# One attention step in eight multiplied in float32 on half-width column tiles

## The chip, the core and the metric

The kernel runs on one core of a Trainium2 chip. The core has five engines that run side by side: PE (TensorE, matrix products into PSUM), DVE (VectorE), ACT (ScalarE), POOL (GpSimd) and SP (SyncE, which here only issues DMAs). Data moves between memory and the core's SBUF by 16 DMA engines. Products land in PSUM, which has eight banks of 512 float32 columns by 128 partitions. The metric is the device time of one execution in microseconds; the profiled execution also gives a span, from its first to its last instruction.

## What is computed

A transformer layer and then a graph attention layer, for 2 sequences of 2048 rows of 512 features, all in float32. The change lies in the first layer's attention (16 heads of 32 features):

```python
q = heads(x @ Wq + bq)
k = heads(x @ Wk + bk)
v = heads(x @ Wv + bv)
scores = jnp.einsum('bhqd,bhkd->bhqk', q, k) / np.sqrt(HD)
attn = jax.nn.softmax(scores, axis=-1)
out = jnp.einsum('bhqk,bhkd->bhqd', attn, v)
...
x = x + out.reshape(B, L, D) @ Wo + bo
mlp = gelu(ada_ln(x, cond, Wln2, bln2) @ W1 + b1) @ W2 + b2
x = x + mlp
```

Each of the 32 (sequence, head) pairs needs 2048 x 2048 scores, their exponentials, and the product of these with the values. The MLP and the graph attention follow.

## The kernel before

**Stages.** A first stage makes the layer norm, the queries, keys and values of the first sequence. Then comes the attention of all 32 pairs, with other work (projections of later heads, the second sequence's norm, the output product of the first sequence) threaded in as a "background" that advances a set number of steps per unit (`PACES`). Then the MLP, and then the graph attention.

**A unit.** A pair has four query blocks of 512, and a query block has eight steps, each with two key tiles of 128. One step is a unit, `u`; there are 32 x 32 = 1024 of them. In unit `u`, `attend` records:

- two score products of 512 columns (`scores`, tile `st`), each into one of three banks, and two exponentials on ACT (`exponents`, tile `e`), which leave float32 exponentials in SBUF;
- two products for the bounds of a later pair's scores (`pair_scores`, tile `mx`), one activation on ACT (`magnitude`, tile `ab`) and one reduction on DVE (`largest`, tile `sums`);
- every fourth unit, one DMA issued by POOL that reads four units of float32 exponentials and writes them back as float16 (`high_parts`, `eh`);
- nine units later, the rest `el = e - eh` in float16, cut along its columns: one part on DVE, the other on POOL (`low_parts`; `SHARES` sets the cut);
- eleven units later, the product with the values (`weigh`): for each of the two key tiles and four groups of 128 queries, `eh` as weights against 65 columns (a column of ones, the high half of the values, their low half) and `el` against 33 (ones and the high half). These 16 matmuls add up in one bank, `av`, over the eight steps. After the eighth, DVE sums the halves, divides by the column of sums and SP stores the result.

**What sets the order.** Every engine call is recorded in the class `Order`, which knows what each reads and writes. `flush` then lays the calls out by a list schedule: a cost for each call (`cost`), a latency from engine to engine, and earlier recorded calls first among those that are ready. Each engine runs its own list in that order, on whose emission nearly all instructions have one line, L269; groups are therefore told apart by their tiles. Calls inside `order.together` stay next to each other; others may be parted. Where a POOL call with two SBUF operands follows a DVE call of that sort, `flush` makes POOL wait for it, so that the two halves of `el` take turns.

**Memory.** `places` gives each tile name a ring of slots in SBUF, and `bank` does so for PSUM. The exponentials `e` have three slots of four units each. All eight PSUM banks are given away: `s0`, `s1`, `s2` to the scores, `x0`, `x1`, `x2` to the bounds, `av` and `misc`.

Of the kernel before, what the change touches and what calls it, by code (L numbers as in the profile page):

```python
# [11 lines left out]
F32 = mybir.dt.float32  # L12
# [10 lines left out]
P = 128  # L23
B, S, D = 2, 2048, 512
KC = D // P
# [9 lines left out]
M = 20  # L35
# [12 lines left out]

EQ = 4

PACES = {0: 0.9, 1: 1.25, 2: 1.25, 17: 0.8, 18: 0.42, 28: 0.55}
# [261 lines left out]
def cost(engine, name, out, ins, kw):  # L313

    n = math.prod(c for _, c in out.ap[1:])
    if name == "dma_start":
        sizes = [mybir.dt.size(a.dtype) for a in (out, ins[0])]
        total = math.prod(c for _, c in out.ap) * max(sizes)
        row = min(a.ap[-1][1] * z if a.ap[-1][0] == 1 else z for a, z in zip((out, ins[0]), sizes))
        row = min(row, 16384)  # L320
        after = total / row * (9 + row / 24.5) / 16
        return (470.0, DONE + after) if engine == "SP" else (1040.0, DONE + 690.0 + after)
    pointers = sum(math.prod(c for _, c in a.ap[1:]) == 1 for a in ins) if n > 1 else 0
    n_in = max([n] + [math.prod(c for _, c in a.ap[1:]) for a in ins])
    psum = any(getattr(a.tensor, "space", None) == PSUM for a in ins)
    if engine == "PE":
        wide = ins[0].dtype == F32
        passes = 1 if not wide else 2 if name == "transpose" else 4
        return max(25.0, n * 0.4167 * passes + 2.7), 0.0
    if engine == "ACT":  # L330
        return (52 if psum else 93) + 0.8325 * n + 93 * min(pointers, 1), 0.0
    if engine == "POOL":
        return (36 + 0.83 * n, 0.0) if not ins else (161 + 0.833 * n, 0.0) \
            if name == "tensor_scalar" else (146 + (1.89 if out.dtype != F32R else 2.1) * n, 0.0)
    fast = name in ("tensor_copy", "tensor_scalar", "memset") and not psum
    return 66 + (0.525 if fast else 1.05) * n_in + 60 * min(pointers, 2), 0.0
# [28 lines left out]
def places():  # L365
# [8 lines left out]
        "wg_b": ["w1"], "x_a": w((7, 9), (2, 4)), "vs_a": ["w4", "eh2", "w0"],  # L374
        "hf_a": ["el0", "el1"], "kf_a": ["h8", "el3"], "hh0": h((0, 4)), "hl0": h((4, 8)),
        "hh1": ["eh0"], "hl1": ["eh1"], "ones": ["el2"],
# [5 lines left out]
        "vs": w((4, 5)), "bv": ["vf1"], "bo": w((6, 7)), "qk2": w((15, 17)), "u2": ["h9"],  # L382
        "wg": w((5, 7)), "x": w((7, 9)), "kf": ["h8"], "uf": ["l1"], "vf": ["vf0"], "qf": ["vf0"],
        "hf": ["vf0"],
        "m2": ["m2_0", "m2_1"], "m1": ["m1_0", "m1_1"], "tr": ["tr_0", "tr_1"],
# [3 lines left out]
        "wo": [f"v{i}" for i in range(4)], "xr": ["vf0", "vf1"], "ob": ["h8", "h9"],  # L389
        "oo2": w((15, 17)), "x1_a": w((7, 9)), "ob_b": ["l9"], "oo2_b": ["v2"],  # L390

        "w": w((4, 6), (7, 9), (2, 4), (14, 15), (11, 13), (9, 10), (15, 17), (10, 11), (13, 14),
               (0, 2)),
        "w8": ["eh0", "eh1"], "w16": q, "gh": h((0, 4), (8, 9)), "gl": h((4, 8), (9, 10)),
        "x1": ["v0", "v1"], "hf_m": ["v3"], "wr": ["ab0", "ab1"] + el[2:4], "gf": el[0:2],
        "g2": ["eh2"], "b2": w((6, 7)), "res": el[2:4] + ["ab0", "ab1"],

        "wbl": ["l0"], "ai": ["l1", "vf0", "vf1"], "af": ["l2"], "cv": ["l3"], "lab1": ["l4", "l5", "l6", "l7"],
        "cvt": ["l8"], "oo": ["l9"],
        "fw": ["vf0", "vf1"], "fv": ["ab0", "ab1"], "fs": ["v2"], "fq": ["l0", "l1", "l2", "l3"],  # L400
        "ws": ["ab0", "ab1"] + el[2:4], "ft": ["v2"],
        "kbd": ["l4", "l5", "l6", "l7"], "gc": ["l4", "l5", "l6", "l7"], "kv": ["l8"], "kh": ["m1_0", "m1_1"],

# [7 lines left out]
def transformer_then_graph_attention(  # L411
# [20 lines left out]
    bank = Slots(order, ps_pool, {  # L432
        "up": ["s0", "s1", "s2", "av", "misc"], "late": ["av", "misc"], "st": ["s0", "s1", "s2"], "mx0": ["x0", "x1"],
        "mx1": ["x2"], "ph": ["x1", "x2", "av"], "gs": ["misc", "s0", "s1"], "gp": ["s2", "x0"],
# [22 lines left out]
    def mm3(acc, lh, ll, rh, rl, start, stop):  # L457
# [14 lines left out]
    gsum = fixed([P, B * NT], "gsum")  # L472
    x40 = fixed([P, KC, B, M], "x40")

# [5 lines left out]
    h_dram = [[dram.tile([2, KC, P, TB], F32, name=f"h_{b}_{tb}", tag=f"h_{b}_{tb}")  # L480
               for tb in range(NTB)] for b in range(1)]
    v_dram = [dram.tile([S, H * VC], F16, name=f"v_{b}", tag=f"v_{b}") for b in range(B)]
    o_dram = [[dram.tile([S, P], F32, name=f"o_{b}_{g}", tag=f"o_{b}_{g}")
# [198 lines left out]

    def norm_block(ps, xt, ln, b, name, hi, lo, tag, stats=None, lows=(V, G)):

# [29 lines left out]
    def first_norm(b, tb, ps, xt, fast, to, stats=None):  # L714
        to[b, tb] = features(b, tb, tb % 2 if fast else 0, "")
        hi, lo = to[b, tb]
        yield from norm_block(ps, xt, 0, b, f"a{b}_{tb}", lambda c: hi[c], lambda c: lo[c],
                              "hf_a" if fast else "hf", stats)
        for v in range(2 if b == 0 else 0):
            if fast and tb % 2:  # L720
                Q.dma_start(out=h_dram[b][tb][v].rearrange("c p t -> p c t"), in_=whole[v].bitcast(F32))
            else:
                for c in range(KC):
                    Q.dma_start(out=h_dram[b][tb][v, c], in_=to[b, tb][v][c].bitcast(F32))
# [8 lines left out]
    def project(b, tb, ps, hi, lo, fast, groups=range(NG), values=True):  # L733
# [72 lines left out]
        def finish_v(t, pp):  # L806
            vs = sb("vs_a" if fast else "vs", [P, H, VC], F16, f"vs_{b}_{tb}_{t}")
            v3 = pp.rearrange("p (h d) -> p h d", d=HD)

            def high():  # L810
                copy(A, vs[:, :, 1:1 + HD], v3)
                G.memset(vs[:, :, 0:1], 1.0)
# [42 lines left out]
    for i in range(2):  # L855
        G.memset(hl_p[i], 0.0)

    heads = [(b, h) for b in range(B) for h in range(H)]
    N = len(heads) * NU
    gates = {}  # L860
    pe = {}
    va, m2s, sts, avs, mxs = {}, {}, {}, {}, {}
    es, ehs, els = [], [], {}

# [20 lines left out]
    def load_values(b, g):  # L885
        va[b, g] = [sb("va" if i < 2 else "va_rest", [P, min(VT, NT - VT * i), 4 * VC], F16,
                       f"va_{b}_{g}_{i}") for i in range(-(-NT // VT))]
        for i, t in enumerate(va[b, g]):
            r = slice(VT * i * P, min(VT * i + VT, NT) * P)
            Q.dma_start(out=t, in_=v_dram[b][r, g * 4 * VC:(g + 1) * 4 * VC]  # L890
                        .rearrange("(t p) c -> p t c", p=P))


# [63 lines left out]
    def high_parts(i):  # L957

        G.dma_start(out=ehs[i % 3], in_=es[i % 3])

    def low_parts(u):
# [3 lines left out]
        G.tensor_tensor(el[:, cd:], e[:, cd:], eh[:, cd:], ALU.subtract)  # L965
        V.tensor_tensor(el[:, 0:cd], e[:, 0:cd], eh[:, 0:cd], ALU.subtract)

    def weigh(u):
# [4 lines left out]
        if kp == 0:  # L973
            avs[0] = bank("av", [P, 4, VC + 1], F32, f"av_{n}_{qb}")
        av = avs[0]
        with order.together("PE"):
            for a in range(2):
                kt = 2 * kp + a
                v = va[b, g][kt // VT][:, kt % VT, hh * VC:(hh + 1) * VC]
                for q in range(4):  # L980
# [4 lines left out]
                    T.matmul(av[:, q, 0:1 + HD], lhsT=el[:, qs], rhs=v[:, 0:1 + HD],  # L985
                             start=False, stop=(kp == 7 and a == 1 and q == 3),
                             skip_group_check=True)
        if kp < 7:
            return
# [37 lines left out]
    def attend(n, work=None):  # L1027

        for u in range(n * NU, (n + 1) * NU):
            i, m = u % NU, u + NU  # L1030
            for a in range(2):
                exponents(2 * u + a)
                if 2 * u + a + 3 < 2 * N:
                    scores(2 * u + a + 3)
            if m < N:
# [5 lines left out]
            if u % EQ == 0 and u:  # L1041
                high_parts(u // EQ - 1)
            if u >= LOW:
                low_parts(u - LOW)
            if u >= WEIGH:
                weigh(u - WEIGH)
# [89 lines left out]

    def second_norm(ps, i, xtag, tag):
        xt = [load(sb(xtag, [P, 2, D], F32, f"x1_{i}_{j}"),
# [5 lines left out]
        def new(to, name):  # L1144
# [3 lines left out]
        yield from norm_block(ps, xt, 1, i // NTB, f"m{i}", lambda c: new(hi, "gh"),  # L1148
                              lambda c: new(lo, "gl"), tag, lows=(V, V))

# [57 lines left out]
    for i in range(3):  # L1208
        es.append(sb(f"q{i}", [P, EQ, 2 * TB], F32, f"e_{i}"))
    for i in range(3):  # L1210
        scores(i)
    beside(some(2, (), True, late), (), 1)
    beside(some(3, (), True, late), (), 1)
    load_values(0, 0)
    for i in range(3):
        ehs.append(sb(f"eh{i}", [P, EQ, 2 * TB], F16, f"eh_{i}"))
# [43 lines left out]
    def from_half():  # L1260
# [3 lines left out]
        yield from output(misc, 0, range(NG), bo_b)  # L1264
        yield from second_norm(misc, 0, "x1_a", "hf")

    works = {0: to_half, 17: from_half, 28: lambda: output(misc, 1, range(NG - 1), from_half.bo_b)}
    for n in range(len(heads)):
# [5 lines left out]
        attend(n, work)  # L1274
    high_parts(N // EQ - 1)
    for u in range(N - WEIGH, N):
        if u + WEIGH - LOW < N:
            low_parts(u + WEIGH - LOW)
        weigh(u)
    work.rest()  # L1280
# [97 lines left out]
    def folded():  # L1378
# [27 lines left out]
        for d in range(2):  # L1406
            for c in range(KC):
# [11 lines left out]
                for fc in range(KC):  # L1419
# [4 lines left out]
                                ALU.add)  # L1424

        g40 = fixed([2, B, M], "g40")
        G.memset(g40, 1.0)
# [15 lines left out]
        for b in range(B):  # L1443
            Q.dma_start(out=rows[b][0:1], in_=cond_dram[b:b + 1])
            Q.dma_start(out=rows[b][1:2], in_=brows[0:1])
        kv = sb("kv", [P, KC, B, M], F32, "kv")
        for fc in range(KC):
# [120 lines left out]
    for i in range(B * NTB):  # L1568
        hi, lo = h2.pop(i)
        nxt = second_norm(misc, i + 1, "x1", "hf_m") if i + 1 < B * NTB else None  # L1570
        held = None
# [216 lines left out]
```

## Time and profile before

| | us |
|---|---|
| median of three runs | 3416.27 (3414.47 to 3421.3) |
| the profiled execution | 3414.05 |
| its span | 3412.0 |
| PE busy in the span | 3183.1 (93%) |
| DVE busy | 2353.7 (69%) |
| ACT busy | 2058.3 (60%) |
| POOL busy | 1536.9 (45%) |

The costliest groups of the attention stage. Each line of the page names the engine, the operation, the tile written and the tiles read, their shape and count, then the busy time and the mean of one in ns, then how long the engine had been idle just before them and what ended most of that.

```profile
L269 POOL TENSOR_TENSOR el<-e,eh 128x496 f16<-128x496 f32 (+2 forms) x1024 | 1153.3, 1146 | 518.7 <-DVE el L269 378.9
L269 ACT ACTIVATE e<-st 128x512 f32<-128x512 f32 x2048 | 1153.6, 618 | 156.5 <-PE st L269 66.0
L269 DVE TENSOR_TENSOR el<-e,eh 128x528 f16<-128x528 f32 (+2 forms) x1024 | 784.5, 810 | 9.3 <-PE av L269 8.9
L269 PE MATMUL av<-va,eh 128*128 128x65 f16 x8192 | 622.9, 193 | 5.4 <-DVE os L269 4.8
L269 PE MATMUL av<-va,el 128*128 128x33 f16 x8192 | 599.6, 181 | 25.1 <-POOL el L269 12.4
```

A matmul's mean is its latency, not the time until the next can start: matmuls overlap, so 8192 of 193 ns have only 622.9 us of busy time between them. The page's DMA part gives the cast `eh<-e` 256 issues of 1024 KB, 8.3 us each from issue to landing, and its queue 40.9% of the time of the 16 DMA engines over the span.

### The profile page before, as it was taken

Reading aid. Unit: us, or ns where it says so; the run is one execution under the profiler, and the core shown is the slowest. Engines: PE = TensorE matmul, PEld = TensorE weight load, DVE = VectorE, ACT = ScalarE, POOL = GpSimd, SP = SyncE. Lnnn points to the kernel's source line nnn. Section 1 sums busy time; section 2 is a strip of 40 time slices with the busy share of each in tenths; the row PEclk is TensorE's granted clock in tenths of the full one; section 3 lists DMA queues with packets and bytes.
Section 4 is the critical chain, followed back from the end, with each engine's and each line's share of the span. In section 5 each row is a group of like instructions: output and inputs, shape, how many; then the busy total and the mean of one; then the engine's idle time right before and its main releaser. Section 6 shows DMA issues by size and latency. Waiting matters only on the chain. (4 is left out here: it accounts for less than half of the span.)

```text
span 3412.0 us, 75509 instructions
## 1 busy us (share of the span) xinstructions
PE 3183.1 (93%) x28042; PEld 2114.2 (62%) x28042; DVE 2353.7 (69%) x5372; ACT 2058.3 (60%) x3984; POOL 1536.9 (45%) x1568
## 2 busy tenths in 40 slices
PE   7988889999999999899998999879999999999999
PEld 5555545555555445455554455558888878788887
DVE  6777667888888887788888887764676324235554
ACT  5777778888888888788888887632221212112111
POOL 2254556666666776676776676641000000003222
PEclk9998999999999999899999999889999999999999
DMA  8998999898989889899998899872222164231111
GB/s 288 266 240 224 233 230 221 188 228 186 219 196 201 173 182 187 176 203 205 190 201 162 162 194 195 189 215 91 63 67 62 33 213 145 64 101 53 56 55 45
DMA packets 358238, 563.35 MB, mean 165 GB/s; under 512 B 127983, under 2 KB 234007, under 8 KB 325102
## 3 DMA queue, kind: packets, MB, share of 16 engines
q0 software_dynamic: 36864, 268.45, 40.9%
q1 hardware_dynamic: 321006, 290.08, 27.7%
q8 instruction: 220, 3.60, 0.4%
q14 instruction: 148, 1.21, 0.1%
HBM read 198.45 MB, written 91.45 MB: 85 GB/s over the span
## 5 line engine op out<-in xcount | busy, mean ns | idle before, releaser
L269 POOL TENSOR_TENSOR el<-e,eh 128x496 f16<-128x496 f32 (+2 forms) x1024 | 1153.3, 1146 | 518.7 <-DVE el L269 378.9
L269 ACT ACTIVATE e<-st 128x512 f32<-128x512 f32 x2048 | 1153.6, 618 | 156.5 <-PE st L269 66.0
L269 DVE CUSTOM_DVE_ANT_0 sums<-mx,ab 128x512 bf16<-128x512 f32 x1024 | 703.4, 687 | 264.6 <-ACT ab L269 203.0
L269 PE MATMUL st<-qst,kst 98*128 98x512 f16 x2048 | 737.4, 389 | 79.1 <-ACT e L269 44.4
L269 DVE TENSOR_TENSOR el<-e,eh 128x528 f16<-128x528 f32 (+2 forms) x1024 | 784.5, 810 | 9.3 <-PE av L269 8.9
L269 ACT ACTIVATE ab<-mx 128x512 f32<-128x512 f32 x1024 | 631.7, 617 | 152.4 <-PE mx L269 131.1
L269 PEld LDWEIGHTS <-eh 128*128 128x128 f16 x8192 | 548.7, 99 | 200.0 <-issue 149.8
L269 PE MATMUL av<-va,eh 128*128 128x65 f16 x8192 | 622.9, 193 | 5.4 <-DVE os L269 4.8
L269 PE MATMUL av<-va,el 128*128 128x33 f16 x8192 | 599.6, 181 | 25.1 <-POOL el L269 12.4
L269 PEld LDWEIGHTS <-el 128*128 128x128 f16 x8192 | 514.9, 97 | 143.8 <-DVE el L269 30.4
L269 PE MATMUL mx<-ust,qst 96*128 96x512 f16 x1024 | 396.0, 387 | 36.9 <-ACT ab L269 23.2
L269 PE MATMUL mx<-kst,qst 96*128 96x512 f16 x1024 | 389.0, 388 | 43.5 <-DVE m L269 41.9
L269 PEld LDWEIGHTS <-qst 96*128 96x128 f16 x2048 | 193.0, 98 | 346.5 <-issue 258.9
L269 ACT ACTIVATE gf<-ph,b_c 128x512 f32<-128x512 f32 x128 | 88.1, 689 | 467.1 <-PE ph L269 406.5
L269 PE MATMUL ph<-gh,w 128*128 128x512 f32 x1024 | 346.5, 400 | 3.1 <-ACT w L269 1.4
L269 PEld LDWEIGHTS <-kst 98*128 98x128 f16 x2048 | 171.4, 98 | 221.6 <-issue 176.9
L269 POOL TENSOR_TENSOR res<-res,b_b 128x512 f32<-128x512 f32 x32 | 42.7, 1348 | 570.2 <-DVE g L269 269.4
L269 PE MATMUL po_s<-w,g 128*128 128x512 f32 x1152 | 297.4, 398 | 0.0
L269 PEld LDWEIGHTS po_s<-w,g 128*128 128x128 f32 x1152 | 214.1, 188 | 49.5 <-issue 2.7
L269 POOL DMA_DIRECT2D eh<-e x256 | 146.2, 571 | 218.2 <-ACT e L269 80.0
L269 DVE CAST g<-gf 128x512 fp32r<-128x512 f32 x128 | 56.4, 441 | 254.5 <-PE po_x L269 243.5
L269 PEld LDWEIGHTS ph<-gh,w 128*128 128x128 f32 x1024 | 192.2, 189 | 51.2 <-issue 3.2
(257 smaller groups left out, 4039.2 us busy)
## 6 DMA issues: line engine op xcount, KB each, us to landing
eh<-e POOLq DMA_DIRECT2D x256, 1024.0 KB, 8.3
wg<-w SPq DMA_DIRECT2D x56, 512.0 KB
x<-in_x SPq DMA_DIRECT2D x24, 512.0 KB
qst<-qk SPq DMA_DIRECT2D x192, 64.0 KB
kst<-qk SPq DMA_DIRECT2D x192, 64.0 KB
x<-xr SPq DMA_DIRECT2D x48, 256.0 KB
v<-vs SPq DMA_DIRECT2D x32, 260.0 KB
qk<-q SPq DMA_DIRECT2D x32, 256.0 KB
```

Of the source, the lines that this page charges most:

```text
L269: ins = call(*args, **kw)
```

## The change

The last of the eight steps of each query block (`KX = 7`) leaves the scheme of high and low parts:

- its exponentials stay float32; the cast of every second group of four units takes three units instead of four, and the step has no `low_parts` and no `weigh`;
- three units after the step, `weigh_whole` multiplies in float32 the other way round: the values (33 columns: ones and 32 features) are the weights, 256 queries stream. The first key tile's result goes to partitions 0 to 32, the second's to 64 to 96, of one bank, `ot`, so the two use different 64-column tiles of the array. Four matmuls, not kept together, and one ACT copy of the 97 x 512 result to SBUF (`xo`, one slot);
- four float32 matmuls in the seventh step's `weigh`, kept together, take `xo` as weights and a 97 x 33 matrix `pick` (two identities, one below the other) as the moving operand. They turn the result round, add the two halves and accumulate into `av`;
- the float32 values of those two key tiles are copied and stored when they are made (`vx`), and loaded per group of four heads (`xa`);
- `ot` takes the bank `s2`, so the scores have two banks, and `scores` is recorded two ahead of the exponentials instead of three;
- the planner's cost counts a float32 matmul of 256 columns at 2.2 passes;
- to find room in SBUF, unused names are dropped from `places` and five tiles used after attention (`cvt`, `oo`, `kv` with `x40`, `ob_b`) move to slots that others also use.

```diff
+KX = 7
+XLAG = 3
...
         passes = 1 if not wide else 2 if name == "transpose" else 4
+        if wide and n == TB // 2:
+            passes = 2.2
...
-        "up": ["s0", "s1", "s2", "av", "misc"], "late": ["av", "misc"], "st": ["s0", "s1", "s2"], "mx0": ["x0", "x1"],
+        "up": ["s0", "s1", "s2", "av", "misc"], "late": ["av", "misc"], "st": ["s0", "s1"], "ot": ["s2"], "mx0": ["x0", "x1"],
...
+            if (tb * TB // P + t) // 2 == KX:
+                vx = sb("vx", [P, D], F32, f"vx_{b}_{t}")
+                A.copy(vx, pp)
+                Q.dma_start(out=vx_dram[b][t % 2 * P:(t % 2 + 1) * P], in_=vx)
...
+        for a in range(2):
+            Q.dma_start(out=xas[g % 2][:, a, :, 1:1 + HD],
+                        in_=vx_dram[b][ts(a, P), ts(g, P)].rearrange("p (h d) -> p h d", d=HD))
...
-        G.dma_start(out=ehs[i % 3], in_=es[i % 3])
+        n = EQ - (i * EQ % 8 + EQ > KX)
+        G.dma_start(out=ehs[i % 3][:, 0:n], in_=es[i % 3][:, 0:n])
...
+    def weigh_whole(u):
+
+        n, qb = u // NU, u % NU // 8
+        b, h = heads[n]
+        ot = ots[0]
+        for i in range(2):
+            for a in range(2):
+                T.matmul(ot[a * P // 2:a * P // 2 + 1 + HD, ts(i, TB // 2)],
+                         lhsT=xas[h // 4 % 2][:, a, h % 4],
+                         rhs=es[u // EQ % 3][:, u % EQ, a * TB + i * TB // 2:][:, 0:TB // 2],
+                         start=True, stop=True)
+        xo = xos[n, qb] = sb("xo", [XR, TB], F32, f"xo_{n}_{qb}")
+        A.copy(xo, ot[0:XR])
...
+        if kp == KX - 1:
+            xo = xos.pop((n, qb))
+            with order.together("PE"):
+                for q in range(4):
+                    T.matmul(av[:, q, 0:1 + HD], lhsT=xo[:, ts(q, P)], rhs=pick, start=False,
+                             stop=False, skip_group_check=True)
...
-                if 2 * u + a + 3 < 2 * N:
-                    scores(2 * u + a + 3)
+                if 2 * u + a + 2 < 2 * N:
+                    scores(2 * u + a + 2)
...
-            if u >= LOW:
+            if u >= LOW and (u - LOW) % 8 != KX:
                 low_parts(u - LOW)
-            if u >= WEIGH:
+            if u >= XLAG and (u - XLAG) % 8 == KX:
+                weigh_whole(u - XLAG)
+            if u >= WEIGH and (u - WEIGH) % 8 != KX:
                 weigh(u - WEIGH)
```

More of the change, by code (lines that the diff above doesn't have):

```diff
@@ L374, in places @@
         "wg_b": ["w1"], "x_a": w((7, 9), (2, 4)), "vs_a": ["w4", "eh2", "w0"],
-        "hf_a": ["el0", "el1"], "kf_a": ["h8", "el3"], "hh0": h((0, 4)), "hl0": h((4, 8)),
+        "hh0": h((0, 4)), "hl0": h((4, 8)),
         "hh1": ["eh0"], "hl1": ["eh1"], "ones": ["el2"],
@@ L382, in places @@
         "vs": w((4, 5)), "bv": ["vf1"], "bo": w((6, 7)), "qk2": w((15, 17)), "u2": ["h9"],
-        "wg": w((5, 7)), "x": w((7, 9)), "kf": ["h8"], "uf": ["l1"], "vf": ["vf0"], "qf": ["vf0"],
-        "hf": ["vf0"],
+        "wg": w((5, 7)), "x": w((7, 9)), "uf": ["l1"], "vx": ["h8"], "xo": ["xo"],
         "m2": ["m2_0", "m2_1"], "m1": ["m1_0", "m1_1"], "tr": ["tr_0", "tr_1"],
@@ L389, in places @@
         "wo": [f"v{i}" for i in range(4)], "xr": ["vf0", "vf1"], "ob": ["h8", "h9"],
-        "oo2": w((15, 17)), "x1_a": w((7, 9)), "ob_b": ["l9"], "oo2_b": ["v2"],
+        "oo2": w((15, 17)), "x1_a": w((7, 9)), "ob_b": ["l0"], "oo2_b": ["v2"],
         "w": w((4, 6), (7, 9), (2, 4), (14, 15), (11, 13), (9, 10), (15, 17), (10, 11), (13, 14),
@@ L394, in places @@
         "w8": ["eh0", "eh1"], "w16": q, "gh": h((0, 4), (8, 9)), "gl": h((4, 8), (9, 10)),
-        "x1": ["v0", "v1"], "hf_m": ["v3"], "wr": ["ab0", "ab1"] + el[2:4], "gf": el[0:2],
+        "x1": ["v0", "v1"], "wr": ["ab0", "ab1"] + el[2:4], "gf": el[0:2],
         "g2": ["eh2"], "b2": w((6, 7)), "res": el[2:4] + ["ab0", "ab1"],
         "wbl": ["l0"], "ai": ["l1", "vf0", "vf1"], "af": ["l2"], "cv": ["l3"], "lab1": ["l4", "l5", "l6", "l7"],
-        "cvt": ["l8"], "oo": ["l9"],
+        "cvt": ["v3"], "oo": ["v2"],
         "fw": ["vf0", "vf1"], "fv": ["ab0", "ab1"], "fs": ["v2"], "fq": ["l0", "l1", "l2", "l3"],
         "ws": ["ab0", "ab1"] + el[2:4], "ft": ["v2"],
-        "kbd": ["l4", "l5", "l6", "l7"], "gc": ["l4", "l5", "l6", "l7"], "kv": ["l8"], "kh": ["m1_0", "m1_1"],
+        "kbd": ["l4", "l5", "l6", "l7"], "gc": ["l4", "l5", "l6", "l7"], "kv": ["v3"], "kh": ["m1_0", "m1_1"],
         "x2t": ["vf0", "vf1", "ab0", "ab1"], "oos": ["l0", "l1", "l2", "l3"], "sc": ["v0", "v1", "v2"],
@@ L472, in transformer_then_graph_attention @@
     gsum = fixed([P, B * NT], "gsum")
-    x40 = fixed([P, KC, B, M], "x40")
     qk_dram = [[dram.tile([2, D, S], F16, name=f"qk_{b}_{w}", tag=f"qk_{b}_{w}")
@@ L481, in transformer_then_graph_attention @@
                for tb in range(NTB)] for b in range(1)]
+    vx_dram = [dram.tile([2 * P, D], F32, name=f"vx_{b}", tag=f"vx_{b}") for b in range(B)]
     v_dram = [dram.tile([S, H * VC], F16, name=f"v_{b}", tag=f"v_{b}") for b in range(B)]
@@ L681, in transformer_then_graph_attention, with norm_block @@
     HOLD = "hold"
-    def norm_block(ps, xt, ln, b, name, hi, lo, tag, stats=None, lows=(V, G)):
+    def norm_block(ps, xt, ln, b, name, hi, lo, stats=None):
         if stats is None:
@@ L717, in first_norm @@
         yield from norm_block(ps, xt, 0, b, f"a{b}_{tb}", lambda c: hi[c], lambda c: lo[c],
-                              "hf_a" if fast else "hf", stats)
+                              stats)
         for v in range(2 if b == 0 else 0):
@@ L856, in transformer_then_graph_attention @@
         G.memset(hl_p[i], 0.0)
+    xas = [fixed([P, 2, 4, 1 + HD], f"xa_{i}") for i in range(2)]
+    for i in range(2):
+        G.memset(xas[i], 1.0)
+    XR = P // 2 + 1 + HD
+    pick = fixed([XR, 1 + HD], "pick")
+    G.memset(pick, 0.0)
+    for r in (0, P // 2):
+        G.tensor_copy(pick[r:r + 1 + HD], ident[0:1 + HD, 0:1 + HD])
     heads = [(b, h) for b in range(B) for h in range(H)]
@@ L862, in transformer_then_graph_attention @@
     va, m2s, sts, avs, mxs = {}, {}, {}, {}, {}
-    es, ehs, els = [], [], {}
+    es, ehs, els, xos, ots = [], [], {}, {}, []
     def put(dst, src, low):
@@ L966, in low_parts @@
         V.tensor_tensor(el[:, 0:cd], e[:, 0:cd], eh[:, 0:cd], ALU.subtract)
+    def weigh_whole(u):
+        n, qb = u // NU, u % NU // 8
+        b, h = heads[n]
+        ot = ots[0]
+        for i in range(2):
+            for a in range(2):
[5 more added lines that the diff above has]
+        A.copy(xo, ot[0:XR])
     def weigh(u):
@@ L985, in weigh @@
                     T.matmul(av[:, q, 0:1 + HD], lhsT=el[:, qs], rhs=v[:, 0:1 + HD],
-                             start=False, stop=(kp == 7 and a == 1 and q == 3),
+                             start=False, stop=(kp == KX - 1 and a == 1 and q == 3),
                              skip_group_check=True)
-        if kp < 7:
+        if kp < KX - 1:
             return
@@ L1135, in transformer_then_graph_attention, with second_norm @@
     h2 = {}
-    def second_norm(ps, i, xtag, tag):
+    def second_norm(ps, i, xtag):
         xt = [load(sb(xtag, [P, 2, D], F32, f"x1_{i}_{j}"),
@@ L1148, in second_norm @@
         yield from norm_block(ps, xt, 1, i // NTB, f"m{i}", lambda c: new(hi, "gh"),
-                              lambda c: new(lo, "gl"), tag, lows=(V, V))
+                              lambda c: new(lo, "gl"))
     h1 = {}
@@ L1209, in transformer_then_graph_attention @@
         es.append(sb(f"q{i}", [P, EQ, 2 * TB], F32, f"e_{i}"))
-    for i in range(3):
+    for i in range(2):
         scores(i)
@@ L1214, in transformer_then_graph_attention @@
     load_values(0, 0)
+    ots.append(bank("ot", [P, TB], F32, "ot"))
+    V.memset(ots[0], 0.0)
     for i in range(3):
@@ L1264, in from_half @@
         yield from output(misc, 0, range(NG), bo_b)
-        yield from second_norm(misc, 0, "x1_a", "hf")
+        yield from second_norm(misc, 0, "x1_a")
     works = {0: to_half, 17: from_half, 28: lambda: output(misc, 1, range(NG - 1), from_half.bo_b)}
@@ L1275, in transformer_then_graph_attention @@
     high_parts(N // EQ - 1)
+    weigh_whole(N - 1)
     for u in range(N - WEIGH, N):
-        if u + WEIGH - LOW < N:
-            low_parts(u + WEIGH - LOW)
-        weigh(u)
+        low = u + WEIGH - LOW
+        if low < N and low % 8 != KX:
+            low_parts(low)
+        if u % 8 != KX:
+            weigh(u)
     work.rest()
@@ L1424, in folded @@
                                 ALU.add)
+        kvx = sb("kv", [P, 2, KC, B, M], F32, "kvx")
+        kv, x40 = kvx[:, 0], kvx[:, 1]
         g40 = fixed([2, B, M], "g40")
@@ L1445, in folded @@
             Q.dma_start(out=rows[b][1:2], in_=brows[0:1])
-        kv = sb("kv", [P, KC, B, M], F32, "kv")
         for fc in range(KC):
@@ L1569, in transformer_then_graph_attention @@
         hi, lo = h2.pop(i)
-        nxt = second_norm(misc, i + 1, "x1", "hf_m") if i + 1 < B * NTB else None
+        nxt = second_norm(misc, i + 1, "x1") if i + 1 < B * NTB else None
         held = None
```

## Prediction

> **What bounds the kernel now.** I read the page's slices first, then a table of stages, then single tiles in one stage, then the order of single instructions. The slices split the run in two. Up to slice 27 all five engines and the DMA engines are loaded; after it PE alone is full. The table of stages (us, then busy time and instructions of PE, weight loads, DVE, ACT, POOL, then granted clock, DMA share, GB/s) says it in numbers:
>
> ```profile
> 600.00:800.00 200.00, 188.93 (x2128) 114.00 (x2127) 164.06 (x378) 169.49 (x341) 124.88 (x133) 1.00 0.90 203
> 1200.00:1400.00 200.00, 183.49 (x2235) 103.98 (x2233) 162.83 (x385) 168.84 (x335) 134.66 (x143) 0.96 0.89 184
> 2600.00:2800.00 200.00, 200.00 (x875) 153.51 (x874) 81.09 (x238) 39.57 (x57) 10.39 (x8) 1.00 0.37 114
> ```
>
> The exponentials run from 127.1 to 2232.3 us and the last subtraction is at 2254, so attention is a stage of 2127 us for 1024 units (a unit: 512 queries against two key tiles), 2.08 us each. The change touches only this stage.
>
> PE's busy time there cannot be used as it stands: it holds the pipeline's latency. The order of instructions gives the spacing of starts, which is what a matmul really takes from PE:
>
> ```profile
> 1003.50 0.38 PE L269 MATMUL mx<-ust,qst 96*128 96x512 f16 x1
> 1003.72 0.38 PE L269 MATMUL mx<-kst,qst 96*128 96x512 f16 x1
> 1003.93 0.20 PE L269 MATMUL av<-va,eh 128*128 128x65 f16 x1
> ...
> 1004.39 0.48 PE L269 MATMUL misc<-hh,wg 128*128 128x512 f32 x1
> ```
>
> A 512-column half-precision matmul takes 0.2165 us, the 16 value matmuls of a unit 0.46 us together (1003.93 to 1004.39, 28.5 ns each), a 512-column background matmul 0.2325 us. Now the same stage, tile by tile (st: PE, ACT; mx: PE, DVE, ACT; misc: PE, loads, DVE, ACT):
>
> ```profile
> 600.00:800.00 200.00, 64.12 (x191) 110.66 (x191) 1.00 0.90 203
> 600.00:800.00 200.00, 63.16 (x193) 65.61 (x96) 60.13 (x97) 1.00 0.90 203
> 600.00:800.00 200.00, 63.81 (x208) 35.84 (x208) 22.37 (x36) 24.36 (x41) 1.00 0.90 203
> ```
>
> (191 + 193) x 0.2165 + 95.5 units x 0.456 + 208 x 0.2325 = 83 + 44 + 48 = 175 us of 200: PE streams 88% of the time where background work is heavy. From 1200 to 1400 the same sum gives 151 us, 79% at its clock of 0.96. Over the stage: 4096 score and bound matmuls 887, values 467, background and the rest about 336, together 1690 us; at the mean clock of about 0.97 that is 1742 us, 82% of 2127.
>
> Nobody else is slack. The two halves of the subtraction el = e - eh take turns on DVE and POOL: DVE's median is 0.697 us, four POOL halves in a row took 4.38 us, so 0.65 + 1.10 = 1.75 us of each 1.87 us unit between 1200 and 1400. ACT is 84 to 87% busy, DMA 89 to 95%. So the stage is balanced: PE is nearest to its end from 600 to 1000 us, the subtraction's turns from 1200 to 1400, DMA before 600 us (0.92 to 0.95).
>
> **What the change takes away**, once per query block (128 of them). Sixteen value matmuls: 128 x 0.456 = 58 us of PE. One subtraction: 128 x 1.14 us of POOL and 128 x 0.77 us of DVE, an eighth of the turns (1.75 falls to 1.53 us per unit). A quarter of every second cast: the cast's queue holds 40.9% of 3412 us for 256 issues, 5.45 us each, so 128 x 5.45 / 4 = 174 us of all 16 DMA engines, 8 points of the stage. These are real reliefs, but of resources beside PE.
>
> **What it adds to PE.** No float32 product of this shape is in the trace, but two near rows are:
>
> ```profile
> 2858.60 1.91 PE L269 MATMUL misc<-fv,kv 128*40 128x512 f32 x4
> 2860.45 0.50 PE L269 MATMUL ph<-gh,w 128*128 128x512 f32 x1
> 2814.15 0.98 PE L269 MATMUL misc<-kv,fw 128*128 128x40 f32 x8
> 2814.96 0.48 PE L269 MATMUL po_s<-w,g 128*128 128x512 f32 x1
> ```
>
> Each float32 matmul is two records. The first row: 4 records of 512 columns, started about 0.44 us apart, so a record takes two passes. With 256 columns a record is 0.2165 us and a matmul 0.433 us; four per block are 1.73 us one after another. They sit on two halves of the columns and may overlap. The Trainium skill ("TensorEngine Tiling (Array Packing)", Key Properties) says that different tiles execute in parallel, but that a change of the tiling mode drains the engine. By its first half the 512 matmuls cost 512 x 0.2165 = 111 us. Its second half speaks against this change: in the order in which the changed program is built, the four are not kept together. I count 331 separate runs of them among full-width matmuls: 222 single ones, 61 pairs, 24 triples, 24 complete fours. The two records of one matmul use the same half and cannot overlap, so I count two slots of 0.2165 for a single, three for a pair, four for a triple, five for four: 96 + 40 + 21 + 26 = 183 us. The trace has a case of the change of mode: the 40-column group is entered and left about 0.1 us late each time (2860.45 against 2858.60 + 4 x 0.4267 = 2860.31). A 36-row matmul in the last stage (3108.79) loses some 0.3 us in both together. 331 x 0.25 = 83 us. Sum 266 us; between 121 us (the changed program's own planner counts 0.237 us per matmul, and no drain) and 219 + 99 = 318 us (no overlap). I take 266, because the built order, not the ideal four, is what runs.
>
> The small products: 512 float32 matmuls, 97 rows by 128 weights, 33 columns. The second row is nearly this shape: 8 records, four matmuls, took 0.81 us to the next start, and 1.01 us by their weight loads. I take 0.9: 128 x 0.9 = 115 us (104 to 129). The planner's formula gives them 0.06 us each, so bundles of 0.9 us stand in PE's order as if they were 0.23 us, and the score matmuls behind them come late.
>
> PE in all: 266 + 115 - 58 = **+323 us**, 0.32 us per unit (167 to 389). From 600 to 800 us, 95.5 units would then need 175 + 30 = 205 us of PE in 200 us: longer even on a PE that never waits. From 1200 to 1400: 151 + 34 = 185 us, at its clock 193 of 200. So PE is the bound nearly everywhere.
>
> **What it adds to ACT.** 128 copies of 97 x 512 from PSUM, as the casts of this size, 0.60 us: 77 us, ACT's stage sum from about 1780 to 1857 us, 87%. Behind each copy stand the next exponentials; the copy waits for the last of the four matmuls, placed about four units after the block's exponentials end.
>
> **Two score banks instead of three.** A bank's round is exponential 0.60, score 0.39 and two handovers, which no row shows alone; at some 0.25 us each, an estimate from the gaps about them, 1.5 us for two exponentials, against 1.87 us per unit. Alone it fits; with a 0.9 us bundle or a drained group ahead of the score it does not, and ACT waits. Bounds: nothing, to 0.2 us per unit (205 us). I take nothing beside the PE bound, since PE is then the later of the two, and keep the rest as a rival.
>
> The rest: four value copies and their stores and 16 small loads on SP's queue (64 KB each, like the 384 query and key loads already there), a few fills before the stage; 0 to 3 us. The moved slots (labels, folded weights, last output) are used where PE is at 200.00 of 200 and the other engines below two thirds; that hides a wait there, and without cover it is a few us.
>
> **Sum.** The stage's PE work is 1690 + 323 = 2013 us, 2075 at clock 0.97. At 100% that is still under 2127, so the result hangs on how full PE can be. The fullest windows reach 88 to 89% today; with subtraction and DMA relieved I take 93%: 2231 us, +104. Profiled execution: 3414.05 (span 3412.0 and 2 around it) + 104 = 3518; the median of the three runs is 2 us above it, so **3520**. At 97% it is +12 (3428), at 89% +204 (3620): the likeliest case's own range.
>
> **Rivals.**
> (a) PE becomes the bound, as above: 3520, chance 0.60.
> (b) Relief wins: the halves overlap fully and drains hide, PE gains only 167 us, (1690 + 167) / 0.97 / 0.97 = 1974 us; then ACT decides, 1857 us at 90% = 2063, so -64: 3352. For it: the subtraction's turns (94% of a unit in the quiet windows) and DMA at 0.95 early. Against: 222 singles, and 600 to 1000 us where PE leads already. It decides only if the four matmuls cost under about 1.2 us per block with all drains. Chance 0.13.
> (c) Both sides cancel, within 7 us of 3416: 0.05.
> (d) Two banks starve ACT on top of (a): another 0.12 us per unit, +123: 3643. For it: ACT already waits 66 us for scores and 131 us for bounds. Against: ACT has 13% to spare. Chance 0.22.
> This kernel's runs lie within 0.2% (7 us) of each other, which is what counts as no change. Faster 0.13, same 0.05, slower 0.82. The range 3400 to 3660 leaves out most of (b) and the upper third of (d).
>
> **What would show it.** After: the attention stage ends near 2360 us; single 256-column records 0.21 to 0.22 us apart, pairs not doubling; groups of pick near 0.9 us; PE's idle share down, DVE and POOL lower, DMA share near 0.8; longer ACT waits for st. Wrong if the stage shortens, or if four products with their drains take under 1.2 us.

## The result and the profile after

The changed kernel takes 3429.22 us in the median of nine runs (3426.9 to 3431.23), the kernel before 3416.27 us in nine runs beside it (3408.68 to 3423.0). The ratio is 1.0039, with a 95% interval of 1.0028 to 1.005: slower by 13 us, where the prediction said 104 us and a range from 3400 to 3660.

The table of stages of the changed kernel, for the windows shown of before (us, then busy time and instructions of PE, weight loads, DVE, ACT and POOL, then clock, DMA share, GB/s):

```profile
600.00:800.00 200.00, 198.15 (x2051) 119.66 (x2050) 154.54 (x352) 170.59 (x344) 106.75 (x115) 1.00 0.82 186
1200.00:1400.00 200.00, 192.06 (x2141) 105.98 (x2142) 145.82 (x361) 169.56 (x336) 115.01 (x125) 1.00 0.79 160
```

PE is busier (198 of 200 us against 189), DVE and POOL are less busy, the DMA share fell from 0.90 to 0.82, and the granted clock, the share of full TensorE speed that the chip allowed, is higher (over the attention stage 0.981 in place of 0.959). The groups of the page say the same:

```profile
L273 ACT ACTIVATE e<-st 128x512 f32<-128x512 f32 x2048 | 1162.2, 617 | 182.9 <-PE st L273 160.5
L273 POOL TENSOR_TENSOR el<-e,eh 128x496 f16<-128x496 f32 (+2 forms) x896 | 1000.4, 1132 | 537.0 <-DVE el L273 238.3
...
L273 DVE TENSOR_TENSOR el<-e,eh 128x528 f16<-128x528 f32 (+2 forms) x896 | 701.0, 814 | 14.3 <-POOL el L273 7.1
...
L273 PE MATMUL av<-va,el 128*128 128x33 f16 x7168 | 512.2, 180 | 2.9 <-DVE el L273 1.7
...
L273 PE MATMUL ot<-e,xa 128*33 128x256 f32 x1024 | 228.7, 392 | 1.4 <-ACT e L273 1.4
```

Read the ends of the lines. PE hardly waits for el any more (2.9 us before these matmuls against 25.1). ACT now waits 160.5 us for scores, against 66.0. That alone does not make PE the late engine, since two score banks without the rest of the change already raise this wait to 134.2 us (experiment 2). The stage, from the first exponential to the end of the last value matmul, took 2148 us against 2129; what follows is the same length within 2 us.

What the new products take from PE is in the order of instructions. Each float32 matmul is two records. A single matmul (x2), a pair (x4) and a whole four (x8), in three cut-outs of the changed kernel's PE:

```profile
1079.39 0.39 PE L273 MATMUL mx<-ust,qst 96*128 96x512 f16 x1
1079.71 0.62 PE L273 MATMUL ot<-e,xa 128*33 128x256 f32 x2
1080.27 0.60 PE L273 MATMUL st<-qst,kst 98*128 98x512 f16 x2
```

```profile
1112.85 0.38 PE L273 MATMUL mx<-kst,qst 96*128 96x512 f16 x1
1113.16 0.63 PE L273 MATMUL ot<-e,xa 128*33 128x256 f32 x4
1113.72 0.39 PE L273 MATMUL mx<-ust,qst 96*128 96x512 f16 x1
```

```profile
1096.44 0.38 PE L273 MATMUL mx<-kst,qst 96*128 96x512 f16 x1
1096.75 1.06 PE L273 MATMUL ot<-e,xa 128*33 128x256 f32 x8
1097.74 0.73 PE L273 MATMUL misc<-wv,hh 128*128 128x512 f32 x2
```

The start of a group comes 0.31 us after the 512-column matmul ahead of it, where 0.215 us is usual: 0.094 us lost on entry. From there to the next start a single takes 0.56 us and a pair 0.56: the second half of the columns is free. Over all groups of the trace the medians are 0.552 us for 222 singles, 0.559 for 61 pairs, 0.984 for 24 triples and 0.991 for 24 fours. With the entry, 0.646, 0.653, 1.078 and 1.085 us; by the means, 238 us in all. So a four costs less than two singles (1.085 against 1.292 us), and the 222 single matmuls of the 512 run as if there were no second half. The small products:

```profile
1111.16 0.98 PE L273 MATMUL av<-pick,xo 97*128 97x33 f32 x8
1111.97 0.20 PE L273 MATMUL av<-va,eh 128*128 128x65 f16 x1
```

Four of them (8 records) take 0.81 us in the median, 0.84 on average, 108 us in all.

### The profile page after: what moved, and what is told of

Read it like the earlier page. It is cut to its first block, busy times and chain, and to the rows that moved or that the text cites. A ratio compares the mean times of both kernels' runs of the same rounds, so it can differ in the third digit from the quotient of the medians.

```text
span 3429.5 us, 75869 instructions
## 1 busy us (share of the span) xinstructions
PE 3327.5 (97%) x28041; PEld 2201.5 (64%) x28042; DVE 2259.7 (66%) x5245; ACT 2117.1 (62%) x4117; POOL 1384.1 (40%) x1445
## 5 line engine op out<-in xcount | busy, mean ns | idle before, releaser
L273 ACT ACTIVATE e<-st 128x512 f32<-128x512 f32 x2048 | 1162.2, 617 | 182.9 <-PE st L273 160.5
L273 POOL TENSOR_TENSOR el<-e,eh 128x496 f16<-128x496 f32 (+2 forms) x896 | 1000.4, 1132 | 537.0 <-DVE el L273 238.3
L273 PE MATMUL st<-qst,kst 98*128 98x512 f16 x2048 | 720.6, 385 | 38.4 <-ACT e L273 27.1
L273 DVE TENSOR_TENSOR el<-e,eh 128x528 f16<-128x528 f32 (+2 forms) x896 | 701.0, 814 | 14.3 <-POOL el L273 7.1
L273 ACT ACTIVATE ab<-mx 128x512 f32<-128x512 f32 x1024 | 637.2, 622 | 71.0 <-PE mx L273 67.2
L273 PEld LDWEIGHTS <-eh 128*128 128x128 f16 x7168 | 473.9, 98 | 131.1 <-issue 86.0
L273 PE MATMUL av<-va,eh 128*128 128x65 f16 x7168 | 528.8, 192 | 0.5 <-DVE os L273 0.5
L273 PE MATMUL av<-va,el 128*128 128x33 f16 x7168 | 512.2, 180 | 2.9 <-DVE el L273 1.7
L273 PEld LDWEIGHTS <-el 128*128 128x128 f16 x7168 | 443.0, 96 | 96.3 <-DVE el L273 9.0
L273 PE MATMUL ot<-e,xa 128*33 128x256 f32 x1024 | 228.7, 392 | 1.4 <-ACT e L273 1.4
```

The source lines that it names most:

```text
L273: ins = call(*args, **kw)
```

## The experiments

In each, the kernel before ran on the same chip; its medians there were 3415 to 3419 us, and "less" and "more" are against these. The diffs are cut (`...`), some lines to the part that differs.

**1. The four products together.**

```diff
+        with order.together("PE"):
             for i in range(2):
                 for a in range(2):
                     T.matmul(ot[...
```

> The changed kernel with its four float32 matmuls of a block kept together, nothing else. Measured in the changed kernel's trace (start of the group to start of the next matmul, plus 0.094 us lost on entry): a single costs 0.646 us, a pair 0.653, a triple 1.078, a four 1.085. All fours would cost 128 x 1.085 = 139 us of PE against 238 now, 99 us less. Theory P (PE is the bound of the changed kernel, 92% full): the time falls by 50 to 100 us, to 3330 to 3380. Rival B (the two score banks hold ACT back, PE is only busy beside it): no change or a loss, 3420 to 3450, since a group of 1.1 us now stands ahead of a score. Rival R (the other engines are just as tight, so PE time is not worth its own length): a gain of under 30 us, 3400 to 3425.

3370.08 us (ratio to before 0.9863, 0.9841 to 0.9884): 59 us under the changed kernel for 99 us less of PE. So PE time counts in the changed kernel, at about 60% of its length, and the version is faster than both kernels (45 us under the one before). All 128 groups of eight records take 0.991 us in the median.

**2. Two score banks alone**, on the kernel before.

```diff
-"st": ["s0", "s1", "s2"]
+"st": ["s0", "s1"]
...
-                    scores(2 * u + a + 3)
+                    scores(2 * u + a + 2)
```

> The kernel before with two score banks instead of three and scores recorded two ahead, nothing else of the change. Theory P: the lookahead costs little, 0 to 20 us, 3416 to 3436. Rival B: it costs 40 us or more, 3456 and up, and then the change without it would have been faster than before.

3445.1 us (1.0085, 1.0061 to 1.0109), 30 us more, between the two expectations. The table of waits (who waited for whom: us in total, times, longest) shows the way it takes:

```profile
ACT e L269 <- PE st L269: 134.2, 228, 4.2
```

In the kernel before this wait was 66.0 us in 92 waits.

**3 and 4. The relief without the price, and the price without the relief.** The third run takes `weigh_whole` and the small products out of the changed kernel; the fourth puts the old treatment of the eighth step back beside the new.

```diff
 # 3
-            if u >= XLAG and (u - XLAG) % 8 == KX:
-                weigh_whole(u - XLAG)
...
-        V.reciprocal(rec, av[:, :, 0])
+        V.tensor_scalar(rec, av[:, :, 0], 0.0, 1.0, ALU.mult, ALU.add)
 # 4
-        n = EQ - (i * EQ % 8 + EQ > KX)
+        n = EQ
...
-            if u >= LOW and (u - LOW) % 8 != KX:
+            if u >= LOW:
```

> The changed kernel without the float32 products: no four matmuls, no copy of their result, no small products; the last step's share is left out of the sums, and the division by them with it (a copy of the same size stands there). What is left is the relief alone, with two banks: PE 1690 - 58 = 1630 us, ACT 1780, an eighth less of subtraction and casts. Theory P: the relief is worth something of its own, 3250 to 3330 (the stage falls by 90 to 170 us), and the products then cost 100 to 180 us. Rival R: the relief is worth nearly nothing since ACT and the score loop hold the stage, 3370 to 3416, and the products cost only 15 to 60 us.

> The changed kernel with the old treatment of the last step put back beside the new one, so that this step is counted twice in the sums: the price without the relief. PE 1690 + 346 = 2036 us. If the relief of the subtraction and the casts is what let PE fill (theory P as the prediction had it, with 88 to 90% as the fullest), 3560 to 3640. If PE can fill to 92% without any relief (its waits were slack all along), 2036 / 0.92 = 2213 us of stage, 3500 at most; under 3470 if it fills to 95%.

The relief alone: 3282.55 us (0.9614, 0.9585 to 0.9643), 133 us less. The price alone: 3602.74 us (1.0542, 1.0514 to 1.057), 188 us more. These two large effects make up the small result: the products cost 147 us where the relief is present (3282.55 to 3429.22), and the relief is worth 174 us where the products are (3602.74 to 3429.22).

How full PE was can be compared over the stage. PE's work is estimated from the products' measured prices, 28.5 ns per value matmul and the 1690 us of the prediction for the rest. The last column divides the share by the clock that was granted over the stage.

| version | PE work, us | stage, us | share | granted clock | share of what was granted |
|---|---|---|---|---|---|
| before | 1690 | 2129 | 79% | 0.959 | 83% |
| relief alone (3) | 1632 | 2000 | 82% | 0.969 | 84% |
| price alone (4) | 2045 | 2324 | 88% | 0.976 | 90% |
| both | 1978 | 2148 | 92% | 0.981 | 94% |
| both, four together (1) | 1879 | 2086 | 90% | 0.980 | 92% |

**5 and 10. The planner's costs.** Costs as measured, with the four together (5) and without (10):

```diff
         if wide and n == TB // 2:
-            passes = 2.2
+            passes = 2.5
+        if wide and n == 1 + HD:
+            passes = 15.5
```

> The changed kernel with its four float32 matmuls together, and with the planner's costs set to what the trace shows: 2.5 passes for a 256-column float32 matmul (0.27 us, a quarter of 1.085) and 15.5 for the 33-column ones (0.22 us, where its formula gives 0.06). If late scores behind bundles that the planner takes for short are a large part of what is left (ACT waits 118 us for scores in the version with the four together), 20 to 40 us under it: 3330 to 3350. If order hardly matters once PE is full, 3360 to 3380.

> The changed kernel with the planner's costs set to the measured ones, but the four float32 matmuls not kept together: in this order there are 124 singles, 44 pairs, 16 triples and 63 fours, which by the measured prices are 80 + 29 + 17 + 68 = 194 us of PE, 44 less than now and 55 more than all together. If time follows PE (59 us for 99), 3400 from grouping alone. If the true costs themselves help as they did beside the grouping (30 us), 3365 to 3385. If they help only where the four are together, 3395 to 3430.

5: 3340.18 us (0.9763, 0.9739 to 0.9788), the best version: 79 us under before and 89 under the changed kernel. 10: 3361.14 us (0.9848, 0.9824 to 0.9872), 68 us under the changed kernel, more than the 44 us of PE that its order saves. The number was expected, its way was not: ACT waits longer for scores in 5 (second line) than in 1 (first line).

```profile
ACT e L273 <- PE st L273: 118.3, 205, 3.4
ACT e L273 <- PE st L273: 141.8, 234, 2.0
```

It waits less for bounds (27.6 us in 5, 50.3 in 1, 67.2 in the changed kernel). Where the 30 us between 1 and 5 come from stays open.

**6. Three score banks, one taken from the bounds**, with the four together.

```diff
-"st": ["s0", "s1"], "ot": ["s2"], "mx0": ["x0", "x1"]
+"st": ["s0", "s1", "s2"], "ot": ["x1"], "mx0": ["x0"]
...
-                    scores(2 * u + a + 2)
+                    scores(2 * u + a + 3)
```

> The changed kernel with its four float32 matmuls together, the scores back to three banks and three ahead; the bank for the result is taken from the bounds instead (one bank for the keys' bounds in place of two). In the kernel before, the third score bank was worth 30 us. If it is worth the same here and the bounds' second bank is worth little, 3335 to 3350. If PE is so full that lookahead no longer counts, 3360 to 3375. If the bounds' second bank is worth more than the scores' third, 3380 and up.

3865.84 us (1.1301, 1.1278 to 1.1324), 496 us over the first experiment: the third expectation's side, and far beyond it. Its waits name the place:

```profile
PE mx L273 <- DVE m L273: 403.5, 456, 2.9
...
ACT ab L273 <- PE mx L273: 315.5, 374, 4.6
```

With one bank, the next keys' bounds cannot start before DVE has read the last ones, and PE stands in order behind them.

**7, 8, 9 and 13. The relief in parts**, each on the kernel before: the subtraction of the eighth step (7), its part of the cast (8), its value matmuls (9), subtraction and cast together (13).

```diff
 # 7
+        if u % 8 == 7:
+            els[u] = last_el[0]
+            return
...
 # 8
-        G.dma_start(out=ehs[i % 3], in_=es[i % 3])
+        n = EQ - i % 2
+        G.dma_start(out=ehs[i % 3][:, 0:n], in_=es[i % 3][:, 0:n])
...
-ehs[u // EQ % 3][:, u % EQ]
+ehs[u // EQ % 3][:, u % EQ - u % 8 // 7]
 # 9
-            for a in range(2):
+            for a in range(2 if kp < 7 else 0):
...
```

> The kernel before, with the eighth step's subtraction left out: its product takes the seventh step's low parts, so PE, casts and ACT stay as they are and only DVE and POOL lose an eighth of el. That step's low part is wrong in the output. If the turns of DVE and POOL hold the stage (1.75 of 1.87 us per unit in the quiet windows), the time falls by 60 to 130 us, to 3290 to 3355. If they are only one of several, by 20 to 50 us. If PE alone, by under 10 us.

> The kernel before, with the cast of every second group cut to three units; the eighth step's subtraction and product take the seventh's high parts, so that step is wrong in the output, and PE, ACT, DVE and POOL do as much as before. It shows the relief of the DMA engines alone (174 us of all 16 less). If the casts hold the stage by their landing, the time falls by 40 us or more, to under 3375, most of it before 600 us where the DMA share is 0.92 to 0.95. If not, 3400 to 3420.

> The kernel before, with the eighth step's 16 value matmuls left out and nothing else (its casts and low parts are still made; the step's share is missing from the sums, and the division by them with it): 58 us less of PE, at 28.5 ns each. Relief alone was worth 133 us with two score banks, which cost 30, so about 163; the casts gave 67 and the subtraction's turns 26. If the reliefs add up, the values are worth the remaining 70: 3345 to 3365. If PE time is worth about its own length, 3355 to 3375 (58 / 0.97 = 60). If it is worth less because PE waits for others, 3380 to 3410.

> The kernel before with the shorter casts and the eighth step's subtraction left out together, its product made of the seventh step's parts (and the division left out, a step of the same size in its place): all of the relief except PE's own 58 us, with three score banks and a planner that knows of it. Relief in all, with PE's and with two banks, was 133 us. If it is the casts and the subtraction together that count, 3290 to 3330. If PE's 58 us are needed for it too, 3340 to 3370.

7: 3392.85 us (0.9922, 0.9895 to 0.9948), 26 less. 8: 3351.48 (0.98, 0.9776 to 0.9825), 67 less. 9: 3409.47 (0.9987, 0.9974 to 1.0001), no difference. 13: 3269.16 (0.9574, 0.9551 to 0.9597), 147 less. Taking 58 us of work from PE alone gained nothing that can be told; taking no work from PE at all, but an eighth of subtraction and cast, gained 147. The windows of the ninth run (one line) and of the thirteenth (two), as in the tables of stages:

```profile
600.00:800.00 200.00, 185.22 (x1899) 109.38 (x1896) 163.65 (x376) 168.35 (x339) 122.35 (x132) 0.97 0.90 204
600.00:800.00 200.00, 191.37 (x2238) 120.58 (x2238) 171.47 (x384) 177.45 (x362) 117.93 (x126) 0.99 0.89 203
1200.00:1400.00 200.00, 188.88 (x2357) 110.94 (x2354) 162.30 (x394) 176.31 (x352) 133.54 (x140) 0.96 0.87 179
```

From 600 to 800 us, where the prediction had PE nearest to its end, the ninth run has 229 PE instructions fewer than the kernel before, and yet DVE, ACT and POOL got no further (376, 339 and 132 instructions against 378, 341 and 133). The thirteenth, with all of PE's work, got through more in the same window: 2238 PE instructions against 2128, and 362 of ACT against 341.

**11, 12, 14 and 15. Work or order?** Every edit makes the planner lay out another order. 11 tells the planner of shorter casts and makes them as before; 12 makes them shorter and does not tell it (`PLAN[0]` scales the size of a DMA in the planner's cost); 14 and 15 only add and take 0.5 ns in its PE costs. 16 and 17 are these two controls on the changed kernel.

```diff
 # 11, around an unchanged cast
+        PLAN[0] = (EQ - i % 2) / EQ
 # 12, around the shorter cast
+        PLAN[0] = EQ / n
 # 14 and 16; 15 and 17 have 2.2
-        return max(25.0, n * 0.4167 * passes + 2.7), 0.0
+        return max(25.0, n * 0.4167 * passes + 3.2), 0.0
```

> The kernel before, doing exactly the same work; only its planner is told that every second cast is a quarter shorter, as it is told in the version with the shorter casts. If that version's 67 us came from the order in which its calls were laid out, this one gains 40 us or more, 3375 and under. If they came from the DMA engines, 3400 to 3435: no gain, perhaps a loss, as casts land later than planned.

> The version with the shorter casts, with its planner told that they are as long as before: the DMA engines have less to do, the planner does not know it. If the 67 us came from the DMA engines, 3345 to 3375; if from the order laid out, 3395 to 3425.

> A control: the kernel before with 0.5 ns added to the planner's cost of every PE call, the work unchanged. The list schedule then comes out in another order (some 2,700 PE rows stand elsewhere, as many as in the runs of single reliefs). How far the time moves is how far the order alone can move it: if under 10 us, the single reliefs of 67 and 26 us stand as they are; if 20 us or more, the 26 us of the turns and the 7 us of the values cannot be told from another order.

> The same control with 0.5 ns taken away. If the order matters little, both controls lie within 10 us of 3416; if one is 20 us or more off, the order's own scatter is that large.

> The same control on the changed kernel: 0.5 ns more in the planner's cost of every PE call. PE is fuller here (92% against 79%), so the order has less slack to hide in; if PE's own time sets the end, this stays within 15 us of 3429. If it moves by 25 us, as the control did on the kernel before, the 13 us between the two kernels are smaller than what the order alone does, and the change itself cannot be called slower.

> The same with 0.5 ns taken away. Both controls near 3429: the change costs what was measured. One of them at or under 3416: the sign of the result belongs to this one order.

| run | us | ratio to before, interval |
|---|---|---|
| 11, new plan, old casts | 3387.71 | 0.992 (0.9895 to 0.9945) |
| 12, old plan, shorter casts | 3405.49 | 0.997 (0.9961 to 0.9979) |
| 14, before, +0.5 ns | 3439.95 | 1.0069 (1.0045 to 1.0093) |
| 15, before, -0.5 ns | 3407.27 | 0.9971 (0.9959 to 0.9983) |
| 16, changed, +0.5 ns | 3419.37 | 1.001 (0.9998 to 1.0023) |
| 17, changed, -0.5 ns | 3427.78 | 1.003 (1.0018 to 1.0042) |

The order alone moves the kernel before by 33 us (3407 to 3440) and the changed one by 10 (3419 to 3429). So the third bank's 30 us, the subtraction's 26 us and the parts of the cast's 67 us (28 from the plan alone, 10 from the shorter casts alone) are no larger than what another order does; 59, 133, 147, 188, 496 and the 79 us of the best version are, as far as three orders of each kernel show it. And the 13 us of the result are smaller: over three orders each, the kernel before has a mean of 3421 us and the changed one of 3425. That these two programs differ by 0.39% is measured; that the change costs anything beyond its order is not shown.

## Why the prediction was wrong

**The step that failed: the price in PE time, in the sum "2013 us of PE, at clock 0.97, with PE at 93%".** All three figures were off, and each made the forecast longer. The sum gave 2231 us for the stage; measured are 2148, some 84 less.

- *PE's work* was 1978 us, not 2013: worth 39 us of the stage.
- *The clock* was 0.981, not 0.97: 25 us. The 0.97 is the whole execution's (0.973); the stage of before had 0.959, and with the products it rose.
- *PE's fullness* was 94% of what was granted, not 93%: 20 us. The 93% was a guess, not worked out from anything, so that it came near is luck.

The other 7 of the 91 us between 3520 and 3429 lie outside the stage and between profiled run and median. Each error is 1 or 2% of the stage, but the forecast was a difference of only 5% of it. The prediction's case "97%: 3428" has the measured number, but not its fullness.

**Price and relief apart.** With its own figures (2013 + 58 us of PE, clock 0.97, 88.5% without relief) the prediction's estimate for the price alone would be 2412 us, 285 more than before, and the relief would then be worth 181 us. Measured over the stage: 195 and 176. So the relief, which stood in the sum only inside the 93% and PE's 58 us, was about right in size; the price was 90 us too large.

**PE's work in parts.** Four products 266 against 238; small products 115 against 108; the removed 58 was priced at the spacing seen before and was not measured again. Within the 266, the drains were too dear: 0.25 us per run, where 0.094 on entry and 0.12 to 0.13 on exit were measured. The prediction's 40-column row had shown about 0.1 us each way; it went above it for the 36-row one. A pair was priced at three slots and a four at five: they take two and four, since the first passes of both halves start 7 ns apart and then the second passes. The built order, with its 222 singles, was rightly taken in place of the ideal one.

**The bound of before (wrong).** "PE is nearest to its end from 600 to 1000 us" made PE the bound of the heavy windows, and their 88 to 89% the fullest that PE gets without relief. It was no ceiling: 58 us less of PE got the other engines no further there (9), an eighth of subtraction and cast gained 147 us (13), and the price alone filled PE to 90% over the whole stage (4). The page had shown the rest (0.94 of the turns in the quiet windows, DMA at 0.89 to 0.95); I called it relief of resources beside PE.

**What held of (a).** With both parts PE's time counts: 99 us less of it gave 59, where 58 us less in the kernel before gave nothing that can be told.

**The Trainium skill's two rules** ("TensorEngine Tiling (Array Packing)", Key Properties) both hold here: the halves overlap, and a change of mode costs 0.21 us per visit. The count of 331 visits decided between them, and keeping the four together removed 203 of those.

**ACT's copy** was 0.60 predicted and 0.589 measured (75 us). **Two banks** as a cost beside PE: 30 us on the kernel before, which its own scatter of order nearly covers; rival (d), 123 us more, did not come. What two banks cost beside the products was not measured: no bank is free for a third, and taking one from the bounds (6) cost far more.

**Rival (b)** put the point at "under about 1.2 us per block with all drains". The block costs 1.86 us, and the kernel was slower by only 13 us; with the four together, 1.085 us, it is faster by 45, and with true costs by 79. That does not contradict the threshold, but it would fit any between these two prices. The gain it named (64 us) lies between the two measured ones; that ACT then decides, as (b) had it, is not shown, for PE was still at 92% of what was granted.

## What to carry to other kernels

A busy engine is the bound only if taking work from it shortens the run; where several stand at 80 to 95%, take an eighth off each, alone and two at a time, before pricing a change by one of them: here the subtraction and the cast gave 26 and 67 us alone, and 147 together. Matmuls on column halves overlap only with a neighbour in the built order, so keep them together. Try a planner with the spacing measured in a trace: here it beat the formula, for a reason that stays open. Where a planner lays out the order, run it with its costs shifted by a hair: differences below that scatter cannot be told from the order's. And where a forecast is a small difference of two long times, errors of 1 or 2% in each factor, the clock's too, can be as long as the change itself.

## What the runs showed of the hardware

Two float32 matmuls on the two column halves run fully side by side: the pair takes 0.559 us to the next start, a single 0.552. A visit to the half-width mode costs about 0.21 us, in and out. The granted clock of the stage went with PE's share of it: 0.912 at 73% (experiment 6: 1879 of 2578 us), 0.959 at 79%, 0.976 at 88%, 0.981 at 92%. From before to after this alone is worth some 2% of PE's time; why it rises is not shown. And the second PSUM bank of a result can be worth far more than the third: one bank in place of two for the keys' bounds cost 496 us, two in place of three for the scores 30.
